# Attention over 154 context rows, then a mixture of experts: the products of the last 26 context rows go from four heads in one block-diagonal product to eight 32x32 squares of the array, the scatters go in pairs, and every step gets a new place

## The chip, the core and the metric

The kernel runs on one core of a Trainium2 chip. The metric is device time of one execution in microseconds (us), the median over several executions. All data is 32-bit floating point. In a profile each 32-bit product is two MATMUL records, each with its own weight load.

## The reference

```python
x = x + xattn(layernorm(x), ctx, Wq, bq, Wk, bk, Wv, bv, Wo, bo)   # x: 2 x 1024 x 256, ctx: 2 x 154 x 256
x = x + moe(layernorm(x), router_w, w1, w2)

# xattn: 16 heads of 16 columns
scores = einsum('bhqk,bhsk->bhqs', q, k) / 4
heads  = einsum('bhqs,bhsk->bhqk', softmax(scores), v)
out    = concat(heads) @ Wo + bo

# moe: 8 experts with 1024 hidden columns, every row takes the best 2 of softmax(x @ router_w.T)
for e in range(8):
    out += w_e[:, None] * (gelu(x @ w1[e].T) @ w2[e].T)
```

## The kernel before

The 2048 rows of x are four chunks (n = 0 to 3) of 512 rows; chunks 0 and 1 belong to the first batch element, 2 and 3 to the second. The kernel is written as some fifty small step functions, all of them Python generators, and a hand-kept list, ORDER (L45), says in which order their parts are issued. A word such as `values.2.1` advances that step by one part. The instructions of TensorE (PE), VectorE (DVE), ScalarE (ACT) and the sync engine's DMA queue (SP) stand in each engine's queue exactly in the order of this list. GpSimd (POOL) does so up to the step `release`; behind it only its dependences and a scheduler order it. So a wait at the head of a queue holds up all that stands behind it.

**Attention, by chunk.** A chunk has two halves (c or half = 0, 1) of eight heads each; a half is two groups (gg = 0, 1) of four heads, and a head of group gg sits with its 16 columns in one of the four 32-row strips of the 128 partitions (j = 0 to 3), the other 16 rows of the strip being zeroed by a mask. `flip_half` transposes the normalized rows, `prep_q` (L348) makes q for both groups. `maxima` (L606) makes the scores with rows as the outputs, eight products of 32x128x154, and DVE takes the maximum over the 154 context rows. `drop` (L630) transposes these maxima, writes them to DRAM (`nm_d`) and reads them back into spare rows of q, so that the next products give scores less their maximum. `exps` (L647) makes these scores for the first 128 context rows with context rows as outputs, four products of 32x128x512 by group, one for each strip; ACT takes the exponential.

The last 26 context rows have steps of their own. `last_keys` (L440) copies their keys into `krem`, a zeroed tensor in which head j of a group has a 32x32 block on the diagonal. `last_exps` (L663) then needs one full 128x128x512 product for each group, two for each half, and one exponential. `values` (L678), by group, starts with one full 128x128x512 product with the block-diagonal `vrem`, whose spare columns are ones (they sum the exponentials), and adds four products of 128x32x512 for the first 128 context rows:

```python
av = ps_one([P, TB * P], f"av{n}_{g}")
nc.tensor.matmul(av, vrem[:, b, g].rearrange("p j k -> p (j k)"), state["er", n, half][:, gg, :], start=True, stop=False)
for j in range(QJ):
    nc.tensor.matmul(av[j * QR : (j + 1) * QR, :], vaug[:, b, g, j, :], state["et", n, g, j // 2][:, j % 2, :], start=False, stop=True)
```

DVE transposes the result to `u`, `divide` (L698) divides by the sums and transposes back, `project` (L715) multiplies with Wo, adds to x and writes x to the output in DRAM.

**PSUM.** Two pools: `ps_two`, three buffers of two banks (scores, exponentials), and `ps_one`, two buffers of one bank (all other products, so `av`, q, projections, router products and transposes).

**Routing.** `second_norm` (L744) writes the normalized rows to `x2n_d`, `logits`, `share`, `choose` and `place` (L832) find the two experts of each row and its place in the table of its expert; `place` ends with the places as integers, `rows_i`. `record` (L849) scatters row numbers and weights into the table `tab_d` in DRAM by two indirect DMAs on POOL for each of the four 128-row blocks of a chunk. `plan` (L867) counts and fixes which expert each tile of 128 table entries uses: once with the first two chunks (word `plan.1`, tiles 0 to 8) and once with all of them.

**Experts, by tile j.** `entries` (L948) reads the tile's table entries by SP, `fetch_weights` (L960) two 512 KB pieces of w1, `fetch_rows` (L972) gathers the rows on POOL, `flip_rows` transposes them, `expand` (L989) and `contract` (L1005) are the two layers in halves, and a scatter on POOL adds the result to the output. 36 tiles always run. w2 of all experts lies in SBUF, loaded by eight `load_w2` of 1 MB each; before that, the parts of experts 6 and 7 hold the normalized and transposed rows of attention.

Of the kernel before, what the change touches and what calls it, by code (L numbers as in the profile page):

```python
# [8 lines left out]
F32 = mybir.dt.float32  # L9
# [5 lines left out]
P = 128  # L15
B, S, D = 2, 1024, 256
H, DK = 16, 16
# [28 lines left out]
warm first_moments.0 first_moments.0 loads.x1 biases flip_context.1 first_moments.0  # L46
first_moments.0 biases loads.wq first_scale.0 prep_norm.0 flip_context.0 flip_context.1
prep_norm.0 flip_context.0 prep_norm.0 prep_norm.0 first_moments.1 flip_half.0.0 flip_half.0.1
flip_half.0.0 flip_half.0.1 first_moments.1 keys.0 keys.0 keys.0 prep_q.0.0 prep_q.0.0
first_moments.1 first_moments.1 prep_q.0.0 loads.wv loads.x3 context_values.1 loads.wo  # L50
maxima.0.0 first_scale.1 loads.bo clear_tables first_moments.3 maxima.0.0 load_w2.3 maxima.0.1
first_offset.1 maxima.0.0 loads.rw keys.1 prep_norm.1 maxima.0.1 prep_norm.1 maxima.0.2
maxima.0.1 context_values.1 context_values.1 prep_norm.1 loads.x2 maxima.0.2 last_context.1
maxima.0.2 prep_q.0.1 keys.1 keys.1 maxima.0.3 last_context.0 prep_q.0.1 maxima.0.3 prep_q.0.1
last_values.0 last_values.0 maxima.0.3 centred_router loads.bias last_values.0 drop.0.0
prep_norm.1 centred_router last_keys.0 maxima.0.4 first_moments.2 flip_half.1.0 flip_half.1.0
last_keys.1 flip_half.1.1 last_values.1 flip_half.1.1 last_values.1 first_moments.2 prep_q.1.0
last_values.1 maxima.0.4 drop.0.0 context_values.0 first_moments.2 prep_q.1.0 exps.0.0
maxima.0.4 prep_q.1.0 first_moments.3 last_exps.0.0 exps.0.0 exps.0.0 maxima.0.5 first_moments.3
first_moments.2 last_exps.0.0 maxima.0.5 flip_output maxima.0.6 constants context_values.0  # L60
maxima.0.5 maxima.0.6 first_scale.2 flip_output context_values.0 maxima.0.6 first_offset.2
exps.0.1 values_bias exps.0.1 maxima.0.7 values_bias values.0.0 first_offset.0 maxima.0.7
maxima.0.7 exps.0.1 prep_norm.2 drop.0.1 values.0.0 maxima.1.0 prep_norm.2 first_moments.3
prep_q.1.1 prep_q.1.1 drop.0.1 maxima.1.0 maxima.1.1 maxima.1.0 load_w2.0 prep_q.1.1 values.0.1
maxima.1.1 own_logits.0 exps.0.2 first_scale.3 values.0.1 maxima.1.1 exps.0.2 prep_norm.2
own_logits.0 output_router maxima.1.2 first_offset.3 output_bias output_router exps.0.2
maxima.1.2 prep_norm.2 maxima.1.3 maxima.1.2 maxima.1.3 maxima.1.3 last_exps.0.1 last_exps.0.1
own_logits.1 drop.1.0 exps.0.3 output_bias flip_half.2.0 own_logits.1 divide.0.0 divide.0.0
values.0.2 flip_half.2.0 drop.1.0 exps.0.3 exps.0.3 values.0.3 values.0.2 exps.1.0 load_w2.2
flip_half.2.1 exps.1.0 maxima.1.4 values.0.3 divide.0.1 output_bias exps.1.0 flip_half.2.1  # L70
maxima.1.4 prep_norm.3 maxima.1.5 divide.0.1 prep_norm.3 prep_q.2.0 maxima.1.5 output_bias
add_bias.0 maxima.1.4 maxima.1.6 maxima.1.6 prep_q.2.0 prep_q.2.0 maxima.1.5 add_bias.1
maxima.1.6 prep_norm.3 project.0.1 project.0.1 exps.1.1 exps.1.1 own_logits.2 maxima.1.7
project.0.0 own_logits.2 exps.1.1 logits.0 maxima.1.7 maxima.1.7 last_exps.1.0 drop.1.1
add_bias.2 prep_norm.3 clear_tables project.0.0 flip_half.3.0 second_moments.0.1 logits.0
last_exps.1.0 maxima.2.0 flip_half.3.0 drop.1.1 second_moments.0.1 values.1.0 maxima.2.0
maxima.2.1 second_moments.0.0 load_w2.5 flip_half.3.1 maxima.2.0 maxima.2.1 flip_half.3.1
values.1.0 second_moments.0.0 exps.1.2 values.1.1 exps.1.2 maxima.2.1 second_scale.0 logits.0
maxima.2.2 maxima.2.2 exps.1.2 prep_q.3.0 maxima.2.3 logits.0 maxima.2.2 values.1.1 maxima.2.3
maxima.2.3 drop.2.0 last_exps.1.1 divide.1.0 prep_q.2.1 last_exps.1.1 prep_q.3.0 prep_q.3.0  # L80
prep_q.2.1 exps.1.3 prep_q.2.1 divide.1.0 values.1.2 exps.1.3 exps.1.3 share.0 share.0 share.0
values.1.3 drop.2.0 exps.2.0 exps.2.0 values.1.2 choose.0 values.1.3 choose.0 last_exps.2.0
exps.2.0 divide.1.1 maxima.2.4 divide.1.1 own_logits.3 maxima.2.4 maxima.2.4 load_w2.1
last_exps.2.0 own_logits.3 maxima.2.5 project.1.1 second_scale.0 maxima.2.5 release maxima.2.6
maxima.2.5 maxima.2.6 maxima.2.6 exps.2.1 project.1.1 second_moments.1.1 logits.1 exps.2.1
exps.2.1 maxima.2.7 maxima.2.7 maxima.2.7 project.1.0 logits.1 maxima.3.0 second_moments.1.1
drop.2.1 values.2.0 maxima.3.0 project.1.0 drop.2.1 maxima.3.1 second_moments.1.0 values.2.1
values.2.0 project.0.0 maxima.3.1 maxima.3.0 prep_q.3.1 exps.2.2 second_moments.1.0 project.1.0
second_scale.1 maxima.3.1 values.2.1 exps.2.2 place.0 logits.1 maxima.3.2 divide.2.0 exps.2.2
divide.2.0 logits.1 maxima.3.2 prep_q.3.1 maxima.3.3 maxima.3.2 prep_q.3.1 maxima.3.3  # L90
second_norm.0 maxima.3.3 drop.3.0 last_exps.2.1 last_exps.2.1 load_w2.6 exps.2.3 load_w2.7
values.2.2 load_w2.4 share.1 second_norm.0 share.1 exps.2.3 drop.3.0 place.0 record.0.0 share.1
exps.2.3 values.2.2 choose.1 values.2.3 choose.1 place.1 exps.3.0 values.2.3 record.0.1
record.0.2 second_scale.1 last_exps.3.0 exps.3.0 exps.3.0 last_exps.3.0 divide.2.1 divide.2.1
maxima.3.4 project.2.0 record.0.3 place.1 maxima.3.4 second_norm.1 project.0.1 maxima.3.5
record.1.0 maxima.3.4 project.2.0 second_norm.1 project.2.1 maxima.3.5 maxima.3.6 maxima.3.5
second_moments.2.0 add_bias.3 record.1.1 second_moments.2.0 project.2.1 plan.1 maxima.3.6
maxima.3.6 project.1.1 second_norm.0 exps.3.1 exps.3.1 second_moments.2.1 record.1.2 maxima.3.7
second_moments.2.1 second_norm.0 second_norm.1 second_scale.2 project.2.0 second_norm.1
maxima.3.7 project.2.1 second_scale.2 record.1.3 second_norm.2 maxima.3.7 second_norm.2  # L100
second_norm.2 exps.3.1 drop.3.1 drop.3.1 second_norm.2 plan.1 values.3.0 values.3.0 values.3.1
logits.2 plan.1 fetch_weights.0 logits.2 exps.3.2 exps.3.2 values.3.1 exps.3.2 last_exps.3.1
entries.0 entries.1 logits.2 exps.3.3 divide.3.0 last_exps.3.1 fetch_rows.0 exps.3.3 values.3.2
# [31 lines left out]
def kernel(  # L135
# [111 lines left out]
    for j in range(QJ):  # L247
        nc.gpsimd.memset(vrem[j * QR : j * QR + SX, :, :, j, DK:QR], 1.0)
# [223 lines left out]
    def last_values(b):  # L472
# [8 lines left out]
        for j in range(QJ):  # L481
# [4 lines left out]
            if j % 2 == 1:  # L486
                yield
# [714 lines left out]
```

## Time and profile before

| | before |
|---|---|
| median of 6 executions | 450.25 us (448.65 to 452.5) |
| the profiled execution | 453.53 us, span 451.8 us |
| PE busy | 425.2 us, 94% of the span |
| weight loads (PEld) | 331.3 us |
| DVE, ACT, POOL busy | 170.2, 125.0, 149.0 us |
| mean granted TensorE clock | 0.972 |
| data moved | 63.75 MB, mean 141 GB/s |

The span runs from the first to the last instruction of one execution. PE and PEld are the matrix products and the loads of their stationary operand; the two overlap. A busy time is the union of its records, and products are pipelined, so the steady price of a group of products is read from the distance between the starts of two groups that follow each other, not from a record's length. "idle before <-releaser" is the time in which an engine waited ahead of an instruction, and who ended the wait.

### The profile page before, as it was taken

The page shows a single profiled execution, that of the slowest core. Times are in us where ns is not written, and L with a number is a line of the kernel's source. Part 1 is how long each engine was busy: PE and PEld are TensorE (multiplying, and loading weights), DVE is VectorE, ACT ScalarE, POOL GpSimd, SP SyncE. Part 2 cuts the span into 40 slices and gives each one's busy share as a digit, 9 for nine tenths or more (in the row PEclk, how much of TensorE's full clock was granted, in tenths as well). Part 3 has the DMA queues.
Part 4 walks back from the last instruction along what each step waited for, and adds up shares of the span by engine and source line. Part 5 has one row for each costly group of instructions (what it writes and reads, how often), then busy time and mean ns, then how long its engine had stood idle before and what let it go on. Part 6 is the DMA issues. An engine that isn't in the chain of part 4 may idle for free. (4 is left out here: it accounts for less than half of the span.)

```text
span 451.8 us, 8169 instructions
## 1 busy us (share of the span) xinstructions
PE 425.2 (94%) x2992; PEld 331.3 (73%) x2992; DVE 170.2 (38%) x435; ACT 125.0 (28%) x206; POOL 149.0 (33%) x166
## 2 busy tenths in 40 slices
PE   7999999999999398999999999999999999999991
PEld 6555545436435127999999899999999999999990
DVE  6766666688888335654210111111111111111100
ACT  3265454363354250541211111121212111121210
POOL 6040124000047213377544343333433333332221
PEclk9899989999999796999999999999999999999997
DMA  7300330220636864799498666767566666761211
GB/s 268 146 9 9 101 107 6 96 100 4 238 151 102 69 217 145 230 222 250 82 292 260 184 160 180 195 163 213 136 202 154 190 170 171 201 156 15 24 15 13
DMA packets 32121, 63.75 MB, mean 141 GB/s; under 512 B 11929, under 2 KB 17617, under 8 KB 31057
## 3 DMA queue, kind: packets, MB, share of 16 engines
q1 hardware_dynamic: 23664, 54.19, 40.1%
q0 software_dynamic: 7936, 8.43, 11.3%
q8 instruction: 26, 0.43, 0.4%
q10 hardware_dynamic: 481, 0.58, 0.4%
q14 instruction: 14, 0.11, 0.1%
HBM read 54.63 MB, written 9.60 MB: 142 GB/s over the span
## 5 line engine op out<-in xcount | busy, mean ns | idle before, releaser
L997 PEld LDWEIGHTS hp<-xgT,w 128*128 128x128 f32 x1152 | 136.7, 195 | 3.6 <-DVE xgT L985 1.8
L997 PE MATMUL hp<-xgT,w 128*128 128x128 f32 x1152 | 138.1, 278 | 1.2 <-DVE xgT L985 1.2
L1013 PE MATMUL yp<-w_sb,hT 128*128 x576 | 130.4, 379 | 0.0
L1013 PEld LDWEIGHTS yp<-w_sb,hT 128*128 128x128 f32 x576 | 106.7, 190 | 13.1
L1002 ACT ACTIVATE hT<-hp 128x512 f32<-128x512 f32 x72 | 42.4, 597 | 215.5 <-PE hp L997 215.5
L1023 POOL DMA_INDIRECT out_dram<-ag,ents x36 | 57.2, 1589 | 111.8 <-DVE ag L1020 87.3
L973 POOL DMA_INDIRECT xg<-x2n_d,ents x36 | 38.0, 1054 | 66.0 <-PE xgt L982 39.6
L1020 DVE TENSOR_SCALAR ag<-yp,ents 128x256 f32<-128x256 f32 x36 | 17.4, 483 | 110.0 <-PE yp L1013 80.3
L621 DVE TENSOR_REDUCE nmx<-mx 128x4 f32<-128x616 f32 x64 | 48.5, 792 | 22.0 <-PE mx L614 21.9
L985 DVE COPY xgT<-xgt 128x256 f32<-128x256 f32 x36 | 15.2, 424 | 100.9 <-PE xgt L982 100.9
L854 POOL DMA_INDIRECT tab_d<-entry,rows_i x32 | 31.0, 969 | 36.0 <-issue 32.6
L659 ACT ACTIVATE et<-st 128x1024 f32<-128x1024 f32 x32 | 31.6, 1024 | 32.0 <-PE st L653 31.8
L614 PEld LDWEIGHTS mx<-kaug,q 32*128 32x128 f32 x512 | 21.3, 185 | 16.3 <-issue 6.2
L614 PE MATMUL mx<-kaug,q 32*128 32x154 f32 x512 | 30.0, 319 | 1.5 <-DVE nmx L621 0.7
L689 PE MATMUL av<-et,vaug 128*32 128x512 f32 x128 | 19.0, 619 | 7.4 <-ACT et L659 7.4
L653 PE MATMUL st<-q,kaug 32*128 32x512 f32 x128 | 22.0, 648 | 0.6 <-DVE nmx L621 0.5
L684 PE MATMUL av<-er,vrem 128*128 128x512 f32 x32 | 17.9, 641 | 0.5 <-DVE num L880 0.5
L596 POOL TENSOR_TENSOR x_sb<-x_sb,bo 128x1024 f32<-128x1024 f32 x4 | 9.4, 2353 | 27.0 <-DVE bo L548 25.9
L689 PEld LDWEIGHTS av<-et,vaug 128*32 128x32 f32 x128 | 2.7, 109 | 20.4 <-issue 10.6
L354 PE MATMUL qp<-w_sb,wq 128*128 128x512 f32 x32 | 17.3, 668 | 0.0
L982 PE MATMUL xgt<-ident,xg 128*128 128x128 f32 x72 | 14.3, 282 | 2.2 <-DMA xg<-x2n_d,ents 2.2
L668 PE MATMUL sr<-q,krem 128*128 128x512 f32 x32 | 15.9, 618 | 0.0
(169 smaller groups left out, 288.7 us busy)
## 6 DMA issues: line engine op xcount, KB each, us to landing
w<-in_w_dram SPq DMA_DIRECT2D x72, 512.0 KB
w_sb<-in_w_dram SPq DMA_DIRECT2D x8, 1024.0 KB
out_dram<-x_sb SPq DMA_DIRECT2D x8, 256.0 KB
x2n_d<-x2n SPq DMA_DIRECT2D x8, 256.0 KB
x_sb<-in_x_dram SPq DMA_DIRECT2D x3, 512.0 KB
ents<-tab_d SPq DMA_DIRECT2D x36, 1.0 KB
xg<-x2n_d,ents POOLq DMA_INDIRECT x36, 4.1
out_dram<-ag,ents POOLq DMA_INDIRECT x36, 3.8
```

The costliest lines, as they stand in the source:

```text
L614: nc.tensor.matmul(sc[j // 2][:, j % 2, gg * SC : (gg + 1) * SC], q[r, gg, i * P : (i + 1) * P], kaug[r, b, 2 * c + gg, :], start=True, st ...
L621: nc.vector.tensor_reduce(out=nmx[c][:, i, 0 : 2 * QJ].rearrange("p (g j) -> p j g", g=2)[:, pair * 2 : pair * 2 + 2, :], in_=sc[pair][:, ...
L653: nc.tensor.matmul(st[j // 2][:, j % 2, :], kaug[r, b, g, 0:SM], q[r, g % 2, :], start=True, stop=True)
L659: nc.scalar.activation(et, st[pair], AF.Exp)
L684: nc.tensor.matmul(av, vrem[:, b, g].rearrange("p j k -> p (j k)"), state["er", n, half][:, gg, :], start=True, stop=False,)
L689: nc.tensor.matmul(av[j * QR : (j + 1) * QR, :], vaug[:, b, g, j, :], state["et", n, g, j // 2][:, j % 2, :], start=False, stop=True,)
L854: ins = nc.gpsimd.indirect_dma_start(out=tab_d, out_offset=bass.IndirectOffsetOnAxis(ap=rows_i[:, i, k : k + 1], axis=0), in_=entry[:, n * ...
L973: nc.gpsimd.indirect_dma_start(out=xg[j % 3], out_offset=None, in_=x2n_d[0 : reach(j), :], in_offset=row_of(j), bounds_check=reach(j) - 1, ...
L997: nc.tensor.matmul(hp[:, q, :], w1t[dc][:, hc * P : (hc + 1) * P], xgT[:, dc, :], start=dc == 0, stop=dc == DC - 1,)
L1002: nc.scalar.activation(hT[:, half * (HC // 2) : (half + 1) * (HC // 2), :], hp, AF.Gelu)
L1013: nc.tensor.matmul(yp, hT[:, hc, :], flat[:, bass.ds(e * (HC * D) + hc * D, D)], start=hc == 0, stop=hc == HC - 1,)
L1023: nc.gpsimd.indirect_dma_start(out=out[0 : reach(j), :], in_=ag[j % 3], in_offset=None, out_offset=row_of(j), bounds_check=reach(j) - 1, o ...
```

## The change

1. `last_exps`: the scores of the last 26 context rows come from eight products of 32x32x512 for each half. Head j of group gg takes the strip j of `kaug` and q as input and puts its result in strip (j + gg) mod 4 of the bank of group gg. `krem` and the step `last_keys` go; `kaug` is padded with zeros to 160 context rows.
2. `values` is issued by half, not by group: it takes both buffers of `ps_one` for the two groups, issues eight products of 32x32x512 with a smaller `vrem` (one block for each strip and group), then for each group four products of 128x32x512 and DVE's transpose. `last_values` copies v in eight small copies on ACT for each batch element, before in four.
3. The exponentials of `last_exps` (`er`) have two buffers, before one.
4. `record`: the integer places are made by DVE for one block at a time, ahead of the block's pair of scatters; before they were made for the whole chunk at the end of `place`.
5. ORDER is a new list. All steps have the same parts but for the above; their order differs on PE, DVE, ACT, POOL and SP.

```diff
-    krem = const.tile([P, B, QG, QJ, QR], F32, name="krem")
+    kaug = const.tile([P, B, QG, SM + QR], F32, name="kaug")
+    nc.gpsimd.memset(kaug[:, :, :, SC : SM + QR], 0.0)
...
 def last_values(b):
...
-        for j in range(QJ):
-            r = slice(j * QR, j * QR + SX)
-            nc.scalar.copy(vrem[r, b, :, j, 0:DK]..., vr_v[r, :, j])
+        for i in range(QJ):
+            r = slice(i * QR, i * QR + SX)
+            for gg in range(2):
+                nc.scalar.copy(vrem[r, b, gg::2, 0:DK], vr_v[r, :, (i - gg) % QJ, gg, :])
...
 def last_exps(n, half):
...
-            nc.tensor.matmul(st[:, gg, :], krem[:, b, g].rearrange("p j k -> p (j k)"), q[:, gg, :], ...)
+            for j in range(QJ):
+                r, i = slice(j * QR, (j + 1) * QR), (j + gg) % QJ
+                nc.tensor.matmul(
+                    st[i * QR : (i + 1) * QR, gg, :], kaug[r, b, g, SM : SM + QR], q[r, gg, :],
+                    start=True, stop=True,
+                )
...
-    def values(n, g):
+    def values(n, half):
...
+        av = [ps_one([P, TB * P], f"av{n}_{half}_{gg}") for gg in range(2)]
+        for gg in range(2):
+            for j in range(QJ):
+                i = (j + gg) % QJ
+                r = slice(i * QR, (i + 1) * QR)
+                nc.tensor.matmul(
+                    av[gg][j * QR : (j + 1) * QR, :], vrem[r, b, half * 2 + gg, :], er[r, gg, :],
+                    start=True, stop=False,
+                )
+        yield
+        for gg in range(2):
+            g = half * 2 + gg
+            for j in range(QJ):
+                nc.tensor.matmul(av[gg][j * QR : (j + 1) * QR, :], vaug[:, b, g, j, :],
+                    state["et", n, g, j // 2][:, j % 2, :], start=False, stop=True)
+            yield
+            nc.vector.transpose(u[:, gg, :], av[gg])
+            yield
...
 def record(n, i):
-        rows_i = state["rows", n]
+        rows, rows_i = state["rows", n]
+        nc.vector.tensor_copy(rows_i[:, i, :], rows[:, i, :])
+        yield
         for k in range(TOPK):
             ins = nc.gpsimd.indirect_dma_start(out=tab_d, ...)
```

Places in the new list that the prediction speaks of (SP's queue, in its order): x of chunk 1, wo, the clearing of the table, two biases, then wq at the start; and at the end of attention: the output of chunk 2's first half, a store of `x2n_d`, `load_w2.5`, `drop.3.1` (its write and two reads), two output stores, a store of `x2n_d`, `load_w2.7`, the table entries of tile 0, a store of `x2n_d`, the entries of tile 5, w1 of tile 0. On PE, the end of attention is: `maxima.3.7`, `project.2.1`, `own_logits.3`, `values.3.0`, `last_exps.3.1`, `exps.3.2`, `values.3.1` with `exps.3.3` inside it, `project.3.0`, `project.3.1`, `flip_rows.0`, `expand.0`. Before, it is `values.3.0`, `values.3.1`, `exps.3.2`, `last_exps.3.1`, `exps.3.3`, `values.3.2`, `values.3.3`, `flip_rows.0`, `expand.0` with `flip_rows.1`, `project.3.0`.

## The prediction

> **What bounds the kernel now.** I read the page first (PE is busy 94% of the span), then the table of stages in 10 us windows, then PE's timeline, then SP's timeline and POOL's at the one place where PE stands still. The windows (stretch, its length, busy time of PE, PEld, DVE, ACT, POOL, then clock, DMA share, GB/s):
>
> ```profile
> 110.00:120.00 10.00, 10.00 (x84) 4.60 (x80) 8.95 (x21) 0.80 (x3) 0.00 (x0) 1.00 0.37 108
> 120.00:130.00 10.00, 9.73 (x68) 4.12 (x68) 8.64 (x22) 7.33 (x10) 0.45 (x1) 1.00 0.73 301
> 140.00:150.00 10.00, 8.56 (x61) 3.29 (x60) 8.62 (x27) 3.60 (x7) 6.60 (x7) 1.00 0.80 107
> 150.00:160.00 10.00, 3.05 (x24) 1.65 (x28) 1.76 (x8) 2.00 (x3) 0.96 (x1) 0.68 0.58 54
> 170.00:180.00 10.00, 8.87 (x44) 8.20 (x44) 5.60 (x14) 0.60 (x1) 3.50 (x3) 0.66 0.47 150
> ```
>
> Attention keeps PE full until 140 us, with DVE close behind. Then comes a hole around 155 us, with the clock at 0.68 and 0.66 in two of its windows. From 180 us the experts keep PE full again until 440. So time is saved by less PE work before 140, or by a smaller hole; the 11 us behind the last product (440.6 to 451.8) stay.
>
> PE's timeline in attention gives the steady prices, from start to start:
>
> ```profile
> 93.84 1.14 PE L653 MATMUL st<-q,kaug 32*128 32x512 f32 x8
> 94.91 1.13 PE L684 MATMUL av<-er,vrem 128*128 128x512 f32 x2
> 95.96 1.07 PE L689 MATMUL av<-et,vaug 128*32 128x512 f32 x8
> 96.96 1.12 PE L684 MATMUL av<-er,vrem 128*128 128x512 f32 x2
> ...
> 100.08 1.98 PE L668 MATMUL sr<-q,krem 128*128 128x512 f32 x4
> 102.00 0.97 PE L614 MATMUL mx<-kaug,q 32*128 32x154 f32 x16
> ```
>
> Four products side by side in four row strips (L653) cost 1.07 us, four in four column strips (L689) 1.00, one full product with vrem (L684) 1.05, two full products with krem (L668) 1.92. Four narrow products cost as much as one full one, so the strips do run side by side.
>
> The hole, on PE, SP and POOL:
>
> ```profile
> 148.53 1.05 PE L689 MATMUL av<-et,vaug 128*32 128x512 f32 x4
> 156.95 1.07 PE L689 MATMUL av<-et,vaug 128*32 128x512 f32 x2 [7.37 <-ACT et L659]
> ...
> 170.61 0.66 PE L982 MATMUL xgt<-ident,xg 128*128 128x128 f32 x2 [2.23 <-DMA xg<-x2n_d,ents]
> 171.79 3.78 PE L997 MATMUL hp<-xgT,w 128*128 128x128 f32 x16 [0.52 <-DVE xgT L985]
> ```
>
> ```profile
> 150.33 0.38 SPq L638 DMA_DIRECT2D nm_d<-nmT  x1
> 157.52 1.15 SPq L641 DMA_DIRECT2D q<-nm_d  x2
> ...
> 161.46 2.84 SPq L950 DMA_DIRECT2D ents<-tab_d  x4
> ```
>
> ```profile
> 166.39 1.04 POOL L973 DMA_INDIRECT xg<-x2n_d,ents  x1 [14.78 <-DMA ents<-tab_d]
> ```
>
> The last `drop` sits at the head of SP for 7.2 us (nm_d issued 150.33, reads issued 157.52; at an earlier `drop` the two are 1.67 apart, 92.19 and 93.86). Behind it in the same queue wait the first w1 and the table entries, although the plan's integers were ready at 151.8 (L919). ACT stands at the same time behind a store of x2n (5.01 us). The size of the hole: from 138.64 (`project.2.1`) to 184.59 (`contract.0`) is 45.95 us; the groups in between, at their steady prices (project 1.92 three times, maxima 0.74 twice, plan 0.32, exps 1.07 three times, values 2.05 four times, router products 0.58 twice, last_exps 1.92, three flips 0.22, three halves of expand 1.80), make 28.1. The hole is 17.8 us.
>
> **Part by part. Octets.** Eight `last_exps` at 1.92 and sixteen vrem products at 1.05 (2.10 by half) become sixteen groups of eight products of 32x32x512. No row shows such a group. Below, it can't be cheaper than one full product, 0.96 (1.92/2): both stream 512 columns twice. Above, two groups of four in turn cost 2 x 1.05 = 2.10. I take 1.15: in one octet no two products share a square, four row strips cost 1.07 and four column strips with four different inputs 1.00, so both kinds of neighbours are seen to run together; 0.1 is for eight more issues. 8 x (1.92 - 1.15) + 8 x (2.10 - 1.15) = 13.8 us less PE work, all of it in the stretch that PE fills; 0.96 would make it 16.8, and 1.40 would make it 9.8.
>
> The rows bear on one open point: L653's four strips write four banks, one each, and L689's four share a bank but read all rows; an octet's four row strips share one bank, in different partitions. The Trainium skill, "TensorEngine Tiling (Array Packing)", section "Gotcha 1: PSUM Pressure", says that different row tiles can't access the same bank at once, which speaks against this change and would make the time 470 (third rival) instead of 432. "TensorE: Matmul & The Clock Gate", Part 3, gives 10.6 times for sixteen 32x32 squares, with a bank for each row strip; no run here shows that.
>
> **DVE and the two buffers.** Ahead of 150 us DVE comes next: 58.2 us busy in the 70 from 80 to 150 (windows). Four of the `last_exps` and nine of the vrem products stand there, so PE needs 4 x 0.77 + 9 x 0.53 = 7.9 less, 62.1. DVE gets 6 more casts in the first two chunks (0.17 each, L845): 59.2, or 95%. No window above has DVE over 8.95 of 10; at that rate it needs 66.1, so 4 us come back. `values` now holds both buffers of `ps_one` until DVE has transposed: behind it on PE wait project, router products and flips, each for at most two transposes of 0.7, 11 us for eight halves if nothing lay between. The list puts exps and maxima there (other pool), so I take 1. Together +5, from +1 to +8.
>
> **The hole.** In the new list the scatters of chunk 0 stand ahead of `place.1`, so of sixteen scatters at 1.27 (129.55 to 150.65) only eight follow it, and the table is complete about 10 us earlier against PE. What is late next:
> - `last_exps.3.1` waits for the last `drop`. From the end of `maxima.3.7` it takes two reductions (1.5), two transposes (0.6), then 3.85 (nm_d 92.19, reads 93.86 plus 1.15, landing 1.0 as from 158.67 to 159.65): 6.0, and up to 3.5 for the 1 MB of `load_w2.5` ahead in the queue (301 GB/s). PE has 1.92 + 0.58 + 3.15 = 5.65 to do meanwhile. It waits 0.3 to 3.9; I take 2.
> - `project.3.0` now comes directly after `values.3.1`; transpose, reciprocal, product, transpose took 171.65 to 174.21, so 2.6. Before, expand hid this.
> - `flip_rows.0`: plan's last part 2.5, issue 1, entries 4.9 (161.46 to 166.39), gather 4.2 (166.39 to 170.61) are 12.6; PE has 10.3 of work from the end of `values.3.0` and the 4.6 of waits above. Covered, unless `load_w2.7` and the stores ahead of the entries cost their 3.5 to 6; I take 1.
> - The half clock took 2.5 (two halves of expand in 3.57 and 2.57, else 1.80); after some 5 us of waits, 2 again.
>
> Together about 8 instead of 17.8: -9.8, from -14 (a hole of 4) to +0 (the old one).
>
> **Edits at no cost.** `krem`'s copies go from POOL (2 x 1.2 us), with some clearing; POOL stood idle then. Eight more copies on ACT (0.2 each, L483) fall where ACT is busy 3.8 to 5.1 of 10 us; uncovered, 1.6. A second `er` buffer takes a wait away. wq is now issued behind wo and the table's clearing; bytes ahead of it grow by 0.4 MB, 1.4 us at 281 GB/s (first window), and PE needs it at 12.84: +0.5, from 0 to 2.
>
> Sum: -13.8 - 9.8 + 5 + 0.5 = -18.1. The profiled execution took 453.5 us in all (1.7 around its span), so 435.4 for it; that execution is 3.3 over the median, so 432 for a median of 450.25. The ends of the terms give 422 to 445 for this case.
>
> **Rivals.**
> 1. Only four squares at once: an octet costs 2.10, the PE work stays (+1.4), DVE isn't pressed (+1), the hole shrinks: -6.9, 443. For it: no row has more than four products side by side.
> 2. The hole stays, another DMA at the head of SP: -13.8 + 5 + 0.5, 442. For it: three 1 MB loads and the stores still stand in SP ahead of the entries, and stores beside scatters crawled (107 GB/s at a share of 0.80, first hole window).
> 3. Slower: the four row strips of an octet take turns at their common bank, the two banks side by side. 4 x 0.96 = 3.84: 8 x 1.92 + 8 x 1.74 = +29.3, less 9.8, plus 0.5: 470. It decides from 2.5 us for an octet, where the loss eats the hole's gain. Against it: L689's four products fill one bank's four quarters at full speed.
>
> **How the numbers follow.** Forecast 57%, rival 1 13%, rival 2 15%, rival 3 12%, and 3% for a hole that grows. The range 421 to 449 takes in the forecast and the first two rivals. Faster by over 0.5% (under 448, about what a measurement of this kernel can tell from no change): nearly all of the forecast and most of the first two, 79%; within, 6%; slower, 15%.
>
> **What would show it.** An octet's start-to-start distance near 1.15 in PE's timeline says the first step is right; 2 or 4 says rival 1 or 3. DVE over 9 of 10 us in the last windows of attention with PE waits on u or nmx shows the second. The wait ahead of `last_exps.3.1`, ahead of `project.3.0` and ahead of the first flip should sum to 5 or 6 us, with the first expand near 155 us, not 171.8. The prediction is wrong if the time is over 449 or if the saving stands elsewhere.

## The result, and the profile after

| | before | after |
|---|---|---|
| median | 450.32 us (446.7 to 454.04) | 469.71 us (465.21 to 475.14) |
| the profiled execution, span | 451.8 us | 469.8 us |
| PE busy; mean granted clock | 425.2 us; 0.972 | 425.3 us; 0.951 |

The changed kernel is slower: ratio 1.0426, interval 1.0399 to 1.0452. Forecast was 432, with 421 to 449.

PE's timeline of the changed kernel (start, length, engine, line, operation, operands, records; idle before, and who ended it):

```profile
88.28 1.09 PE L668 MATMUL sr<-q,kaug 32*32 32x512 f32 x16
89.29 0.65 PE L567 MATMUL lxp<-w_sb,rwp 128*32 128x128 f32 x16
...
90.94 1.09 PE L689 MATMUL av<-er,vrem 32*32 32x512 f32 x16
91.95 2.13 PE L697 MATMUL av<-et,vaug 128*32 128x512 f32 x16
...
124.75 1.06 PE L697 MATMUL av<-et,vaug 128*32 128x512 f32 x8
135.89 2.09 PE L651 MATMUL st<-q,kaug 32*128 32x512 f32 x8 [10.07 <-DMA q<-nm_d]
...
269.96 0.66 PE L989 MATMUL xgt<-ident,xg 128*128 128x128 f32 x2 [5.45 <-DMA xg<-x2n_d,ents]
```

An octet (the eight products of 32x32x512 of one half of a group) costs 1.01 us from start to start, in scores (88.28 to 89.29) and in values (90.94 to 91.95): all eight run at once. So the change does on PE what it says. The two waits are new. The first stands in the middle of attention (`exps.3.0`), the second in the experts' part. In the table of stages (stretch, length, busy time of PE, PEld, DVE, ACT, POOL, clock, DMA share, GB/s):

```profile
120.00:130.00 10.00, 5.10 (x48) 0.77 (x32) 6.92 (x22) 5.29 (x7) 2.05 (x3) 1.00 0.70 124
130.00:140.00 10.00, 4.11 (x20) 1.68 (x20) 0.64 (x3) 1.94 (x4) 0.00 (x0) 0.53 0.09 30
140.00:150.00 10.00, 9.84 (x74) 5.82 (x71) 7.18 (x15) 2.98 (x5) 2.79 (x3) 0.50 0.07 26
...
260.00:270.00 10.00, 4.55 (x34) 4.02 (x34) 0.00 (x0) 1.08 (x2) 6.31 (x5) 0.86 0.99 324
```

From 125.8 to 135.9 PE stands, and for most of that time the other engines stand with it. Behind it PE is full, but at a clock of 0.50: by the trace's clock record half clock lasts for 20.5 us from 130.6 us on, 5.3 of them still idle and 15.2 with products. SP's timeline and POOL's show what PE waited for:

```profile
111.14 0.42 SPq L272 DMA_DIRECT2D w_sb<-in_w_dram  x1
111.62 0.45 SPq L763 DMA_DIRECT2D x2n_d<-x2n  x1
112.11 0.46 SPq L738 DMA_DIRECT2D out_dram<-x_sb  x1
119.89 0.32 SPq L636 DMA_DIRECT2D nm_d<-nmT  x1
133.74 1.17 SPq L639 DMA_DIRECT2D q<-nm_d  x2
```

```profile
112.29 0.95 POOL L861 DMA_INDIRECT tab_d<-entry,rows_i  x1 [1.85 <-DVE rows_i L858]
...
125.70 0.96 POOL L861 DMA_INDIRECT tab_d<-entry,rows_i  x1 [0.30 <-issue]
```

`drop.3.0` wrote its maxima at 119.89, and its reads could be issued at 133.74, 13.9 us later (1.67 at the undisturbed `drop` of before). The scatters of chunk 0 run at that time (pairs from 107.98 to 125.70; in the old list none before 129.55), beside a 1 MB load and two stores. In the trace's packet records the load's 8 KB packets take 0.31 us alone and 0.3 to 3.5 us here (means of the single microseconds from 112 to 122), and the scatter issued at 112.29 has its last landing at 128.65. The write's own packets stand in the records from 123 to 128.6 us and no packet of any transfer from 129 to 135, yet its last landing is recorded at 133.68, between those of the scatters issued at 119.18 (133.50) and at 124.44 (133.85).

SP's table of waits (who waits for what, us in all, times, longest) names the second new hole:

```profile
SPq L639 <- DMA nm_d<-nmT: 25.2, 8, 13.5
SPq L957 <- DMA tab_d<-entry,rows_i: 24.0, 2, 19.0
```

The entries of tile 9 wait 19.0 us for the second table: the last scatter is issued at 241.63, before at 213.52. Where the time stands can be read off PE's timeline by landmarks (start of the first contraction, of the contraction of the 19th tile, and of the last product; us):

| | first | 19th | last product | first to 19th |
|---|---|---|---|---|
| before | 184.6 | 319.0 | 441.4 | 134.4 |
| after | 189.5 | 336.8 | 459.2 | 147.3 |

From the 19th tile on both take 122.4. Of 17.8 us more, 4.9 arise up to the first contraction, and 12.9 in the experts' first half. The split hangs on the execution of the kernel before: in its second profile (the run `before_again` below, span 447.9) the first contraction starts at 180.7 and 134.3 us pass to the 19th, which makes it 8.8 and 13.0.

### The profile page after: what moved, and what is told of

Read it like the earlier page. It is cut to its first block, busy times and chain, and to the rows that moved or that the text cites. A ratio compares the mean times of both kernels' runs of the same rounds, so it can differ in the third digit from the quotient of the medians.

```text
span 469.8 us, 8570 instructions
## 1 busy us (share of the span) xinstructions
PE 425.3 (91%) x3184; PEld 328.7 (70%) x3184; DVE 171.7 (37%) x447; ACT 128.9 (27%) x216; POOL 145.7 (31%) x158
## 5 line engine op out<-in xcount | busy, mean ns | idle before, releaser
L1004 PEld LDWEIGHTS hp<-xgT,w 128*128 128x128 f32 x1152 | 134.5, 192 | 5.3 <-DVE xgT L992 2.2
L1004 PE MATMUL hp<-xgT,w 128*128 128x128 f32 x1152 | 136.1, 276 | 2.3 <-DVE xgT L992 1.2
L1020 PE MATMUL yp<-w_sb,hT 128*128 x576 | 133.0, 383 | 0.6 <-DVE ag L1027 0.5
L619 DVE TENSOR_REDUCE nmx<-mx 128x4 f32<-128x616 f32 x64 | 48.6, 792 | 20.6 <-PE mx L612 20.5
L992 DVE COPY xgT<-xgt 128x256 f32<-128x256 f32 x36 | 15.2, 423 | 103.1 <-PE xgt L989 103.1
L612 PEld LDWEIGHTS mx<-kaug,q 32*128 32x128 f32 x512 | 24.2, 203 | 20.7 <-issue 7.9
L612 PE MATMUL mx<-kaug,q 32*128 32x154 f32 x512 | 34.8, 347 | 2.5 <-ACT et L657 0.9
L651 PE MATMUL st<-q,kaug 32*128 32x512 f32 x128 | 24.1, 721 | 10.1 <-DMA q<-nm_d 10.1
L651 PEld LDWEIGHTS st<-q,kaug 32*128 32x128 f32 x128 | 7.0, 206 | 22.2 <-issue 17.3
L729 PE MATMUL op<-wo,catT 128*128 128x256 f32 x64 | 17.4, 418 | 2.0 <-DVE catT L720 2.0
L729 PEld LDWEIGHTS op<-wo,catT 128*128 128x128 f32 x64 | 12.5, 206 | 6.0 <-DVE catT L720 2.5
```

The lines of the kernel that those rows point to most:

```text
L612: nc.tensor.matmul(sc[j // 2][:, j % 2, gg * SC : (gg + 1) * SC], q[r, gg, i * P : (i + 1) * P], kaug[r, b, 2 * c + gg, 0:SC], start=True, ...
L619: nc.vector.tensor_reduce(out=nmx[c][:, i, 0 : 2 * QJ].rearrange("p (g j) -> p j g", g=2)[:, pair * 2 : pair * 2 + 2, :], in_=sc[pair][:, ...
L651: nc.tensor.matmul(st[j // 2][:, j % 2, :], kaug[r, b, g, 0:SM], q[r, g % 2, :], start=True, stop=True)
L729: nc.tensor.matmul(op[:, ii, :], catT[:, c, i * P : (i + 1) * P], wo_sb[:, c, :], start=c == 0, stop=c == DC - 1,)
L1004: nc.tensor.matmul(hp[:, q, :], w1t[dc][:, hc * P : (hc + 1) * P], xgT[:, dc, :], start=dc == 0, stop=dc == DC - 1,)
L1020: nc.tensor.matmul(yp, hT[:, hc, :], flat[:, bass.ds(e * (HC * D) + hc * D, D)], start=hc == 0, stop=hc == HC - 1,)
```

## The experiments

One thing has to be known to read the numbers: the chips are of two kinds for this kernel. The kernel before took 450.0 to 450.9 on two of them, as in the result, and 468.1, 473.3 and 472.5 on three others. Every ratio is against the kernel before on the same chip; "450" and "470" name the kind. Each chip was used for one set of runs only, so whether the chip itself or its condition at the time makes the kind is not shown, and on the last of the 470 chips one of eleven executions of the kernel before took 462.2.

### The parts of the change (450)

Octets alone. The old list (without `last_keys`) and `values` by group; the first group of a half takes both buffers and issues the octet.

```diff
-                nc.tensor.matmul(st[:, gg, :], krem[:, b, g]..., q[:, gg, :], ...)      # last_exps
+                for j in range(QJ): ...  # eight 32x32x512, as in the change
-        nc.tensor.matmul(av, vrem[:, b, g]..., er[:, gg, :], ...)                       # values
+        if gg == 0:
+            for k in range(2): state["av", k] = ps_one(...)   # both buffers, then eight 32x32x512
```

> The kernel before with the octets alone: last_exps and values as changed, both buffers of the av pool taken at the first group of a half; ORDER, record and the one er buffer as before. Theory 'the new order costs': the octet is worth its 15 us here (8 x (1.92 - 1.01) + 8 x (2.10 - 1.01)), of which DVE takes back up to 4, so 435 to 440. Rival 'the octets cost' (narrow products leave the clock at half speed for longer, or two av buffers make PE wait for DVE): 450 or more.

Measured: 448.95 us, ratio 0.9969 (0.9939 to 1.0000). PE's timeline:

```profile
122.77 2.21 PE L683 MATMUL av<-er,vrem 32*32 32x512 f32 x16
...
131.77 1.99 PE L721 MATMUL op<-wo,catT 128*128 128x256 f32 x8
```

`project.2.0` starts at 131.77, before at 135.98. Up to there seven halves of scores and six of values have lost 7 x (1.92 - 1.01) + 6 x (2.10 - 1.01) = 12.9 us of PE work; 4.2 us arrive. Five of the six octets of `values` take 1.40 to 2.64 from start to start (the six lose 4.8 us over 1.01): their second four products start 0.4 to 1.2 us behind the first four. These need the second buffer of `ps_one`, which `project` or a transpose can still hold; the trace names such a wait once (0.59 us, for DVE's copy out of it), and for the others it is inferred. Smaller waits for DVE's `u` and ACT's exponentials come on top. Of the 4.2 the medians keep 1.8 (450.77 to 448.95), with an interval that reaches 1.

The list alone: the new ORDER and pairs, with the old full products (`krem` and `last_keys` back behind the keys, one `er` buffer).

```diff
-    (octets in last_exps and values)
+    (the full 128x128x512 products of before; last_keys.c behind the last word of keys.c)
```

> The kernel after, its order and its scatters in pairs, with the full 128x128 products of before in last_exps and values (krem and last_keys again, vrem block-diagonal, one er buffer). Theory 'the new order costs': slower than after, since 15 us of PE work come back, part of it under waits: 475 to 485. Rival 'the octets cost' (half clock after narrow products): 450 to 470, with fewer windows at half clock.

Measured: 471.24, ratio 1.0501 (1.0416 to 1.0586). The list carries the whole loss. By the medians octets give back 1.5 us of it (471.24 to 469.71), by the ratios 3.4, but the intervals overlap, so their gain in the new list is not resolved.

### Edits of the list that should mend one hole (450)

```diff
-... record.2.0 ... record.2.0 record.2.1 ... record.2.1 ... record.2.3   (pairs among the experts' words; so record.3)
+... record.2.0 record.2.0 record.2.1 record.2.1 ... record.2.3 record.2.3   (all at the place of the first)
```

> The kernel after, but the four record steps of chunk 2 stand together, and those of chunk 3, right where the first of each stood, so that POOL does eight scatters in a row. Theory 'scatters in pairs behind the experts' scatters make the second table late': the read of the entries of tile 9 moves from 244 us to about 225, the 9.5 us of PE waits between 220 and 285 and 2 us of half clock go: 458 to 461. Rival 'the entries wait for something else (a full DMA queue)': within 2 us of 469.7.

Measured: 467.36, ratio 1.0403 (1.0329 to 1.0476). Only 2 us less, and these lie inside the intervals. The gathers of the next tiles now stand behind eight scatters, a new hole from 190 to 200 us (PE busy 3.08 of 10), and the entries still wait 15.2.

```diff
-... drop.3.0 last_exps.2.1 record.0.2 values.2.0 load_w2.6 divide.2.0 ... drop.3.0 choose.1
+... drop.3.0 last_exps.2.1 record.0.2 values.2.0 divide.2.0 ... drop.3.0 load_w2.6 choose.1
```

> The kernel after, but the load of w2 of expert 6 (1 MB) is issued right behind the reads of drop.3.0 instead of three DMAs ahead of it. Theory 'the 1 MB load at the head of the queue holds up drop.3.0': nm_d lands 2 to 4 us after its issue instead of 13.9, the 10.1 us wait ahead of exps.3.0 and some 6 us of half clock go: 452 to 458. Rival 'DMA crawls because scatters and stores run, whatever load is there': nm_d still takes over 8 us and the time stays within 3 us of 469.7.

Measured: 466.5, ratio 1.0373 (1.0307 to 1.0440). SP waits 9.7 us instead of 13.5:

```profile
116.58 0.32 SPq L632 DMA_DIRECT2D nm_d<-nmT  x1
126.68 1.10 SPq L635 DMA_DIRECT2D q<-nm_d  x2
```

From the write to the reads it is still 10.1 us with the load out of the way: the load alone doesn't hold the maxima. The 3.2 us less in the median are not clear of noise.

### Scatters or stores? (470)

```diff
-place.0 ... record.0.0 drop.2.1 ... record.0.1 ... record.0.2 ... record.0.3 ... drop.3.0 choose.1
+place.0 ... drop.2.1 ... drop.3.0 record.0.0 record.0.0 record.0.1 record.0.1 record.0.2 record.0.2 record.0.3 record.0.3 choose.1
```

> The changed kernel with one group of list words moved: chunk 0's four casts and eight scatters stand together behind drop.3.0's DMAs, where the changed list has them in pairs between 108 and 126 us, beside the stores of x2n and of the output and ahead of drop.3.0. Theory (scatters beside the 2 KB-row stores slow all DMAs; drop.3.0's nm_d store stands behind them for 13.9 us instead of 1.7): with no scatter in flight before 120 us, nm_d lands within 2 to 4 us, exps.3.0 no longer waits 10.07 us, much of the 20.5 us at half clock goes: 10 to 15 us less, 455 to 460. Rival (the stores and weight loads alone fill the queues; scatters only share the place): exps.3.0 waits 8 us or more as before, 468 to 471.

```diff
-... project.1.0 ... second_norm.0 ... project.0.0 drop.3.0 choose.1      (their stores, ahead of the last part of drop.3.0)
+... drop.3.0 project.1.0 second_norm.0 project.0.0 choose.1
```

> The changed kernel with three stores moved in SP's queue: the two output stores (project.1.0, project.0.0) and the x2n store (second_norm.0) that stand ahead of drop.3.0 are issued behind its reads; the scatters stay. Theory that it takes stores and scatters together: with the stores gone nm_d lands within 2 to 4 us and the time falls by 10 to 15 us, to 455 to 460. Rival (the scatters alone slow every DMA, or the 1 MB weight load beside them does): nm_d still takes 8 us or more, 466 to 471. If this and the moved scatters both mend it, it is the two together; if only one does, that one.

SP's timeline with the scatters moved, and with the stores moved:

```profile
119.89 0.32 SPq L632 DMA_DIRECT2D nm_d<-nmT  x1
121.48 1.17 SPq L635 DMA_DIRECT2D q<-nm_d  x2
```

```profile
116.51 0.33 SPq L632 DMA_DIRECT2D nm_d<-nmT  x1
127.41 1.15 SPq L635 DMA_DIRECT2D q<-nm_d  x2
```

Without scatters in flight the write is through after 1.59 us, with the load and all stores ahead of it; without the stores it still takes 10.9. The changed kernel itself takes 11.9 on such a chip (116.17 to 128.04 in the run `after_again` below). On a 450 chip it is the same: in the run `scatters0_experts_again` below, which has these scatters behind `drop.3.0`, the write is through after 1.6 us (116.19 to 117.80) for 13.9 in the changed kernel. So the write is late only with scatters in flight, and in every such run other transfers were in flight too; scatters alone beside the write were not tried. Times: 463.57, ratio 0.988 (0.9836 to 0.9924), and 467.69 (four executions: 462.4, 463.4, 472.0 and 472.2), no ratio. By time alone the two edits can't be told apart; the traces do it. The first time lies between the two expectations: the wait went, but DVE halted for 7.5 us from 132.8 us on, with ten scatters in a row (126.01 to 137.74).

```diff
-(the changed list behind its first contraction)
+(the words left over, in the order of the old list)
```

> The changed kernel with its own list up to the first contraction (all of attention, first table, first flips) and the old list's order for everything behind it: the scatters of chunks 2 and 3 stand as the old list has them against the experts' gathers and output scatters. Theory (the second table is late because the new list puts pairs of scatters behind the experts' output scatters; tile 9's entries are issued at 244.4, 27.5 later than before, and PE loses about 9.5 us from 220 to 300): entries of tile 9 by about 235 and 6 to 10 us less, 460 to 464. Rival (the table is late only because attention ends late, and the hole moves with it): 468 to 471.

Measured: 462.95, ratio 0.989 (0.9837 to 0.9943). Entries of tile 9 at 233.95 as expected, but the changed kernel was not run on this chip; see the next group.

Octets in the old list, with the last `drop` early:

```diff
-... second_norm.2 maxima.3.7 second_norm.2 second_norm.2 exps.3.1 drop.3.1 drop.3.1 second_norm.2
+... exps.3.1 maxima.3.7 drop.3.1 drop.3.1 second_norm.2 second_norm.2 second_norm.2 second_norm.2 project.0.1 project.1.1 project.2.0 project.2.1
```

> The old list with octets (448.95), its hole mended on three queues: exps.3.1's last part on ACT and both parts of drop.3.1 stand ahead of second_norm.2, and four output stores (project.0.1, 1.1, 2.0, 2.1) are issued behind drop.3.1's DMAs. Theory (octets save PE time, but the routing chain behind the last drop, held by stores beside scatters, takes it back): exps.3.2's wait for ACT (5.65 us) goes to under 2, the reads of drop.3.1 are issued 2 to 4 us after its store instead of 7.8, and the time falls by 4 to 8 us, to 441 to 445. Rival (the first flip is bound by table, entries and gather, which none of this moves): 447 to 450.

Measured: 468.6, ratio 1.0004 (0.9969 to 1.0038). `drop.3.1`'s write was through after 1.6 us, but stood at 157.47 because DVE had halted 7 and 5.6 us earlier in the row of scatters. Inconclusive for a 450 chip, on which it was not run.

### The same kernels on one 470 chip

No edit (the changed kernel), octets alone, chunk 0's scatters moved, and these with the old order of the experts:

> The changed kernel, nothing edited, run beside the next three on one chip. In the last four runs the kernel before took 468.1 us instead of 450.8, so those times need their own base. If this run's kernel before is near 450, the changed kernel should be 468 to 471, ratio 1.043. If it is near 468 again: were the loss a fixed 20 us of the new order, it would be 488; if the slower transfers that hold the old list there are the same that hold the new one everywhere, 468 to 474, ratio 1.00 to 1.01.

> The old list with octets once more (448.95 beside 450.77 before). Theory: octets take PE work out, but the routing chain behind takes it back, so ratio 0.990 to 1.000 on any chip. Rival: the small gain was chance, ratio over 1.000.

> The changed kernel with chunk 0's casts and scatters behind drop.3.0, once more beside the unedited changed kernel. In its first profile drop.3.0's store landed for its reads after 1.6 us instead of 13.9, but a new stall stood at 130 to 140 us, while the ten scatters ran beside stores of x2n. Theory (scatters in flight with any other transfer hold whatever waits for DMA): 3 to 8 us below the changed kernel on the same chip, the rest taken back by the new stall. Rival (no matter where the scatters stand): within 2 us of it.

> The changed kernel with both edits: chunk 0's casts and scatters behind drop.3.0, and the old list's order for all behind the first contraction. Theory (two separate causes, one in attention, one in the experts' part): the gains add, 8 to 14 us below the changed kernel on the same chip. Rival (one wait hides the other): no more than the better of the two alone, 3 to 8 us below.

Measured against 473.3: 467.21, ratio 0.9895 (0.9820 to 0.9971); 469.54, 0.9944 (0.9899 to 0.9989); 463.96, 0.9853 (0.9781 to 0.9926); 456.45, 0.9657 (0.9569 to 0.9745). Here the changed kernel is faster than the one before. It takes about the same on both kinds of chip; it is the old list that loses some 20 us on this one. (The kernel before was profiled again only on a 450 chip, so octets in the old list stand in for it.) That kernel, traced on both kinds, shows where (windows on the 450 chip, on the 470 chip, and DVE's timeline on the latter):

```profile
140.00:150.00 10.00, 4.40 (x40) 0.97 (x36) 5.96 (x23) 3.22 (x9) 4.80 (x5) 0.99 0.71 89
```

```profile
140.00:150.00 10.00, 2.19 (x14) 1.79 (x15) 0.80 (x1) 0.02 (x1) 6.69 (x7) 0.51 0.42 75
```

```profile
146.96 0.80 DVE L613 TENSOR_REDUCE nmx<-mx 128x4 f32<-128x616 f32 x1 [12.90 <-remote]
```

DVE stands for 12.9 us while POOL issues sixteen scatters in a row (128.03 to 148.52); "remote" means that the profile has no instruction or transfer that ended the wait. The first contraction comes at 189.1 instead of 177.5, and from there to the tenth tile's 78.0 us pass instead of 67.9, across the second row of scatters. In the traces of the 470 chips such waits of DVE, of 2.5 to 12.9 us, stand wherever eight or more scatters are issued in a row; with scatters in pairs the longest is 1.0 us, and the ten traces of 450 chips have none. What halts DVE there is not shown.

Moving the scatters of chunk 0 and then restoring the experts' order, one after the other, takes the changed kernel down by 3.3 and 7.5 us. The 10.8 in all lie in the 8 to 14 of the theory of two causes and beyond the rival's 3 to 8. That each keeps its worth without the other is not shown: the old order of the experts alone was not run on this chip, and the 3.3 are not clear of noise.

### Does it hold on a 450 chip?

The kernel before for its profile; both edits; both with chunk 0's pairs spread over the words behind `drop.3.0`; and octets in the old list with scatters in pairs:

```diff
-drop.3.0 record.0.0 record.0.0 record.0.1 record.0.1 record.0.2 record.0.2 record.0.3 record.0.3 choose.1 values.2.1 ...
+drop.3.0 record.0.0 record.0.0 choose.1 values.2.1 exps.3.0 values.2.1 record.0.1 record.0.1 choose.1 record.0.2 record.0.2 ... values.2.1 record.0.3 record.0.3
```

```diff
 # old list with octets
-record.n.i                       (integer places for the whole chunk in place, two scatters)
+record.n.i record.n.i            (a cast of its own on DVE, two scatters)
```

> The kernel before, nothing edited, for its profile on this chip. If this chip gives about 450 us: the hole of the first profile, drop.3.1's reads 7 us behind its store, DVE without a halt. If it gives 468 or more: theory says that the 20 us stand between 130 and 230 us, as DVE halts of 7 to 13 us and half clock while rows of eight scatters run; rival: they are spread evenly (a slower DMA or clock everywhere).

> The changed kernel with chunk 0's casts and scatters behind drop.3.0 and the old order of the experts' part, once more (456.45 where the changed kernel took 467.2 and the kernel before 473.3). If the two causes stand on every chip: 454 to 460 here too. On a chip where the kernel before takes 450, that is a ratio of 1.01 to 1.02, so more than half of the 20 us are given back. Rival: on such a chip it stays near 470.

> As the last one, but chunk 0's four pairs of scatters behind drop.3.0 are spread over the next words (behind its DMAs, a transpose of values.2.1, choose.1, another transpose), so that pauses stand between them. Theory (a long row of scatters is what halts DVE, PE waiting for it 6 us at 130 to 140 us): that wait goes, 3 to 6 us less than with the row, 450 to 454. Rival (any scatters beside the x2n stores do it): within 2 us of the row.

> The old list with octets, and the scatters of all chunks in pairs, each pair behind a cast of its own on DVE (the changed kernel's record); the list is otherwise the old one. Theory: where rows of scatters halt DVE (kernel before at 468 or more), pairs take 3 to 10 us off octets alone (ratio 0.994 to before); where they don't (kernel before at 450), 446 to 450, as octets alone. Rival (pairs cost, as the casts queue the scatters behind DVE): 2 us or more above octets alone.

Measured against 450.87: 450.0, ratio 0.9986 (0.9945 to 1.0027); 455.8, 1.0120 (1.0041 to 1.0199); 457.74, 1.0157 (1.0070 to 1.0243); 454.74, 1.0098 (1.0064 to 1.0132). Three things follow.

The two edits take the changed kernel from 4.3% to 1.2% over, on this kind too: 14 us of the 19.4. By the landmarks 5.8 of them come up to the first contraction (183.7 for 189.5) and 8.6 from there to the 19th (138.7 for 147.3); there 4.4 more than in `before_again` remain. Spreading the pairs gains nothing.

Pairs cost 5.8 us in the old list ((1.0098 - 0.9969) x 450), and the place is the second table: SP waits 17.6 us for it, PE stands at 230 us, and from the first to the 19th contraction 142.4 us pass instead of 134.3.

```profile
SPq L951 <- DMA tab_d<-entry,rows_i: 17.6, 1, 17.6
```

```profile
230.00:240.00 10.00, 3.31 (x23) 3.15 (x22) 0.78 (x2) 0.60 (x1) 1.91 (x2) 0.71 0.72 183
```

What is left in the kernel with both edits is again one `drop`, on SP and on PE:

```profile
136.45 0.32 SPq L632 DMA_DIRECT2D nm_d<-nmT  x1
152.26 1.15 SPq L635 DMA_DIRECT2D q<-nm_d  x2
```

```profile
138.86 1.92 PE L693 MATMUL av<-et,vaug 128*32 128x512 f32 x16
154.19 2.61 PE L664 MATMUL sr<-q,kaug 32*32 32x512 f32 x16 [13.40 <-DMA q<-nm_d]
```

PE has finished `values.3.0` at 140.8, in the kernel before not until 158.9, and then waits 13.4 us, since sixteen scatters (122.30 to 145.43), two stores and a load cross the write of `drop.3.1`. So the PE time of the octets does reach this point, and is spent on a DMA.

### The last `drop` cleared (470)

```diff
-... drop.3.1 second_norm.1 record.1.2 ... load_w2.5 ... record.1.3 drop.3.1 ...      (record.1.0, record.1.1, project.2.0 ahead)
+... drop.3.1 drop.3.1 record.1.0 record.1.0 ... record.1.3 record.1.3 second_norm.1 project.2.0 load_w2.5 ...
```

and, in the second, the casts of chunks 2 and 3 directly behind `place.2` and `place.3`.

> As scatters0_experts_again, with drop.3.1's DMAs directly behind its transposition, and chunk 1's casts and scatters, one store of x2n, one of the output and load_w2.5 behind them. Theory: the store lands for the reads after 2 to 4 us instead of 15.8, last_exps.3.1's wait of 13.4 us falls to under 3; chunk 1's scatters then end near 149, entries and gather end near 161, so the first flip (170.3) comes 6 to 10 us earlier: 446 to 450 where the kernel before takes 450. Rival (the table is now late and takes it all back): 454 to 458.

> As the last one, and the casts of chunks 2 and 3 stand directly behind place.2 and place.3, so that POOL's pairs don't wait for DVE's place in the experts' order; the scatters' own places stay. Theory: the second table is complete 5 to 10 us earlier, and the 5 us that PE loses at 230 to 240 go: 3 to 5 us below the last one, 441 to 446 where the kernel before takes 450, faster than both kernels. Rival (POOL waits for its own output scatters, not for the casts): within 1 us of the last one.

Measured against 472.46: 464.3 and 466.28, without an interval. The write of `drop.3.1` is through after 3.5 us (143.88 to 147.36), but on a 470 chip it had taken only 4.7 in the kernel with both edits. The first gather (171.15) now waits for a store of x2n and the entries come at 166.39, 4.8 later than there: the rival's case, a late table, on this kind of chip. The second table is early with the early casts (last scatter issued at 219.81 instead of 234.96), and the hole behind it is gone (PE is busy all of the time from 230 to 250 us, where the first of the two kernels has 14.85 of 20). But the second loses 5.4 us of PE between 190 and 230, where eight scatters in a row (186.86 to 196.72) go with a halt of DVE:

```profile
198.47 0.48 DVE L1023 TENSOR_SCALAR ag<-yp,ents 128x256 f32<-128x256 f32 x1 [12.73 <-remote]
```

Whether either would gain on a 450 chip was not tried and stays open.

No kernel here beats both everywhere by a clear margin. Octets in the old list are best on the 450 chips (448.95) and 0.6% faster than before on a 470 chip; the changed kernel with both edits is best on a 470 chip (456.45).

## Why the prediction was wrong

**Octets: right, and cheaper than forecast.** 1.01 us for 1.15, so 8 x 0.91 + 8 x 1.09 = 16.0 us less PE work for 13.8. Rival 1 (four at once, 2.10) is refuted, and so is rival 3: its 470 is the measured time, but by chance, since nine of the changed kernel's sixteen octets take 1.01 or 1.02, and the others 1.11 to 3.66 where a wait or the half clock falls in. The rule of the Trainium skill ("TensorEngine Tiling (Array Packing)", section "Gotcha 1: PSUM Pressure") that row tiles can't access a common bank at once isn't borne out here: four row strips of an octet write different partitions of one bank at full speed.

**DVE and the two buffers: mis-sized.** +5 was forecast; octets alone give back 8.7 of 12.9 before the last stage begins. In the changed kernel `last_exps.2.1` starts at 119.82 for 124.27 before: of 10.0 us of PE work saved up to there 4.4 arrive, so 5.5 are given back by then. The buffers were put at 1 of up to 11, with the argument that the new list has exps and maxima behind `values`. There, up to the second half of chunk 2, the octets of `values` lose 2.9 us over 1.01 (three of six take 1.02 to 1.11), against 4.8 in the old list, where `project` stands behind some of them: the order helps, but doesn't bring the loss to 1.

**The hole at the end of attention: smaller, but not by as much as forecast.** These are its parts on PE:

```profile
154.47 1.99 PE L729 MATMUL op<-wo,catT 128*128 128x256 f32 x8
...
163.14 1.06 PE L668 MATMUL sr<-q,kaug 32*32 32x512 f32 x8 [2.48 <-DMA q<-nm_d]
164.94 1.93 PE L668 MATMUL sr<-q,kaug 32*32 32x512 f32 x8 [0.74 <-DMA q<-nm_d]
...
176.42 3.29 PE L729 MATMUL op<-wo,catT 128*128 128x256 f32 x14 [2.05 <-DVE catT L720]
...
189.50 3.91 PE L1020 MATMUL yp<-w_sb,hT 128*128 x16
```

From `project.2.1` to the first contraction 35.0 us pass. At the prediction's own prices for steady work this stretch holds 22.6 us of products, which leaves a hole of 12.4, for 8 forecast and 17.8 before (14.1 in the second profile of before). Of the waits that were forecast, `last_exps.3.1` takes 3.2 us (2 forecast), `project.3.0` 2.05 (2.6) and the flip none (1); half clock costs 1.7 (2). The rest lies in smaller waits, the longest 1.70 for a copy by DVE, and in groups that take longer than their steady price.

**The step that failed: the scatters of chunk 0 were taken as pure gain.** The text counted them so ("the table is complete about 10 us earlier") and followed only the last `drop` through SP's queue; for `drop.3.0`, past which the scatters had moved too, the sum holds nothing. There the write took 13.9 us instead of 1.67. That costs 10.1 us of idle PE, and 15.2 us of products at half clock, 7.6: 17.7, as much as the whole hole that the change was to shrink. The gain was smaller too: against PE the first table came 4 us earlier, not 10 (the last scatter into it is issued 8.1 us behind the start of `project.2.1`, before 12.0). The row that told it was quoted: stores beside scatters at 107 GB/s and a share of 0.80. It was held for a feature of the place, not of the scatters. Summed up to the first contraction: -16.0 + 8.7 - 5.4 + 17.7 = +5.0, for 4.9 measured between the two profiles. That it closes so well is partly luck, since against the second profile of before 8.8 are measured, and the 8.7 come from the run with the old list.

**The experts' part was not priced at all.** "Scatters in pairs" was costed where the first table is made. For chunks 2 and 3 the pairs wait for a cast in DVE's queue, which stands behind the experts' work, and POOL takes output scatters between them. The second table is 28 us later and 12.9 us are lost, 9.5 of idle PE between 220 and 280 us and 3.4 by half clock; in the old list pairs alone lose 8.1 at this place, and with the order restored and the scatters moved 4.4 of the loss are left.

Rival 2 came nearest in kind, a DMA at the head of SP, but as a hole that stays, not as a second one.

**What held and what didn't, of the signs named:** octets at 1.15 or less, yes; DVE over 9 of 10 in the last windows with PE waiting, in part (9.12 from 100 to 110 us, where PE is full, 8.68 from 110 to 120, and PE's waits for `u` and for the maxima stand before 70 us, at most 0.6 us each); the three waits at 5 to 6 us in all, yes (5.3), but as 3.2, 2.05 and none; the first expand near 155 us, no: the first flip stands at 179.7, since all behind `drop.3.0` was late.

**Slips in the prediction's sums.** A product of `vrem` gets 0.48 us cheaper (half of 2.10 less 1.15), not 0.53, so PE has 7.4 us less ahead of 150 us, not 7.9. The terms' ends give 420 to 450, not 422 to 445. And the 3.3 us by which the profiled execution of before lies over the median stand in the very hole that was to shrink (17.8 for 14.1 in the second profile), so taking them off besides counts a part twice. None of this changes the sign of the forecast.

## What to carry to other kernels

When DMAs that many small packets make up are moved, price them against every transfer on whose landing an engine waits, not only against the stage that consumes them: here 14 us for a write that takes 1.6 alone. When work is taken off the engine that looks full, first ask what the next two engines in the loop have left, and which buffers come free in time: beside a DVE busy for 83% of a stretch, DVE, the two buffers and ACT's exponentials together took back two thirds of the 12.9 us saved. And a cast in front of each scatter ties GpSimd to the place of that cast in DVE's queue.

## What the runs showed of the hardware that was not expected

- A 64 KB write that lands in 1.6 us takes 10 to 16 us while scatters of 64-byte packets and other transfers are in flight, though the DMA engines are mostly idle (share 0.09 from 130 to 140 us in the changed kernel, 0.06 from 120 to 130 us with the stores moved). The Trainium skill, "DMA: Bandwidth & Descriptors", section "Queues, rings and completion order", says that an engine takes turns between its queues by packet; that alone would not explain the delay, least of all the last 5 us ahead of the write's landing in the changed kernel, in which no packet is on record. Its section "Specifications" says that below 512 B a transfer is done as read-modify-write; the scatters' packets lie below that, but no run here tells whether it is the cause.
- Half clock lasted 20.5 us around a stall of PE of 10 us, with PE full at half clock for the last 15 of it; so it did in the run `scatters_together`, and 17.1 us in `w26_behind_drop` and `experts_old_order`.
- Chips of two kinds: the kernel before takes about 450 us on one and 470 us on the other; on the second, DVE halts for up to 13 us while eight or more scatters are issued in a row. Whether this belongs to the chip or to its condition at the time is not shown. The sign of a change can turn on it: 1.0426 on one kind, 0.9895 on the other.
